# Second stage's short convolution: from diagonal matmuls to scaled evictions and GpSimd additions, with the first stage's weight loads issued ahead

## The chip, the cores and the metric

One core of a Trainium2 chip runs the whole program. The metric is device time in microseconds (us), the median of several runs. The engines are called as in the profile: PE (TensorE), DVE (VectorE), ACT (ScalarE), POOL (GpSimd), SP (SyncE, which here only issues DMAs). [...]

## What is computed

Four layers follow each other on an image tensor of 4 x 192 x 64 x 64, in fp32: a pair of mambas, a block with one mamba and a convolution, a convolution with weights made from the image, and a layer of sedenion products in 4 x 4 windows. The change touches the second layer's mamba, and a preparation of weights for the fourth layer. The mamba, cut to what matters (`xm` is 384 channels wide, D_CONV is 3, the convolution is per channel and causal):

```python
xz = jnp.einsum('blc,ec->ble', xf, in_proj_w)
xm, z = jnp.split(xz, 2, axis=-1)
conv = jax.lax.conv_general_dilated(xm_t, conv1d_w, (1,), [(D_CONV - 1, 0)],
    feature_group_count=D_INNER, dimension_numbers=('NCH', 'OIH', 'NCH'))
xm = jax.nn.silu(jnp.transpose(conv + conv1d_b[None, :, None], (0, 2, 1)))
x_dbl = jnp.einsum('bld,ed->ble', xm, x_proj_w)      # dt, B, C
delta = jax.nn.softplus(jnp.einsum('blr,dr->bld', dt, dt_proj_w) + dt_proj_b)
# h = exp(delta*A) * h + delta*xm*B ;  y = sum_n h*C  (a scan over the sequence)
y = ys + xm * Dskip
y = y * jax.nn.silu(z)
return jnp.einsum('bld,cd->blc', y, out_proj_w)
```

The first layer's two mambas have the same form with four taps.

## The kernel before

The program has three stages. `two_mambas` is the first layer. `mamba_block` is the second layer. `conv_and_windows` is the third and fourth.

**Units and ticks.** In the first two stages a unit is 512 positions of one sequence for one mamba: 64 units in the first stage, 32 in the second. Channels lie on the 128 partitions; 384 channels are three groups `d`. Of 384 x 16 states, 12 rows `k` of 4 tiles `j` are scanned one tile at a time (`step`, L574, DVE), so a unit is 48 scan steps. I call a scan step a tick. For each tile ACT makes the decay `dA` in PSUM (L568), two ticks ahead of the scan; three PSUM buffers hold it. For each row DVE forms the product with B (L561), and after its fourth tile POOL saves the state (L589) and multiplies by C (L590, `read`); four ticks later PE sums over the states (L599, `sum`). The `h` tiles have three buffers.

**What goes on behind the scan.** All other work is written as generators that yield a `Piece` ahead of each step, and the class `Behind` issues these steps between the ticks. It has four lanes, each a queue: lane 0 spreads C and runs `back` (output projection); lane 1 runs `front` of the next unit and then the first norm of the unit after; lane 2 runs `tail` (depthwise convolution, gelu, second norm); lane 3 runs `end` (the MLP). A piece states its PE time, the ticks to wait, what must be done first, whether it needs one of the two PSUM banks of that pool (`bank=True`), and whether it is a burst (an activation with another table, only allowed in one tick of four). Each tick adds 2.1 us of PE time to a budget in the second stage. A PSUM result's eviction is not issued with its matmul but through `later`, one tick on for ACT, two for DVE; its bank counts as held until then. The order of the instructions is thus fixed when the program is built; if data that a tick needs is not yet issued, `force` issues the lanes' steps until it is (the rows of the next unit are wanted at tick 36).

**The front before.** `front` projects the three groups with PE (L452, three banks), ACT copies each into `raw` behind two columns of the previous unit (`halo`, L448, L480), and nine matmuls with diagonal weights (`m_conv`, made at the start of the stage on DVE, L431) sum the three shifted copies in PSUM (L470, three banks). ACT evicts with the bias (L475) into `xc`, and a burst takes the silu over all three (L482). `xc` has two buffers; the convolution's pieces wait for `u["free"][:1]`, the flag that the unit before the present one has read its `xc` (set in tick 5). Then come the projection to dt, B and C (L486, L488), dt (L496, L499), its softplus (L505), its product with xc on POOL (L506), both stored to DRAM (`r_dt`, `r_dtx`, L511) from where `load` (L531) spreads the rows, and the gate z (L455, silu L523).

**Walsh weights.** `walsh_weights` runs once, at the start of the first stage, ahead of the first unit's front in SP's queue. For each of four pieces SP loads `w_raw` (L904; tag "h", three buffers), DVE takes four passes (L913, L923) between two result buffers (tag "h_apart"), and SP stores the result (L927).

Of the kernel before, what the change touches and what calls it, by code (L numbers as in the profile page):

```python
# [14 lines left out]
F32 = mybir.dt.float32  # L15
AF = mybir.ActivationFunctionType
ALU = mybir.AluOpType
# [5 lines left out]
C = 192  # L23
# [4 lines left out]
ND = DI // 128  # L28
# [4 lines left out]
T = 512  # L33
# [6 lines left out]
NP = NPOS // 2  # L40
# [134 lines left out]
class Behind:  # L175
# [19 lines left out]
        self.held += 1  # L195
        return self.psum.tile(shape, F32, name=name, tag="mm")

    def later(self, fn, dve=False, bank=True):
        done = [False]
        self.pending.append((self.now + (self.dve if dve else self.act), fn, done, bank))  # L200
        return done

    def issue(self, everything=False):
# [198 lines left out]
class Mamba:  # L402
# [1 line left out]


    def __init__(
        self, nc, name, taps, ins, const, last, scan, work, psum_y, psum_a, dram, ident, ex, behind, shared=()
    ):


        self.behind, self.y_free, self.shared = behind, True, shared
        self.nc, self.name, self.taps, self.ex = nc, name, taps, ex
        self.last, self.work, self.psum_y, self.psum_a = last, work, psum_y, psum_a
        self.dram = dram
        pack, pack_ap, in_w_ap, dt_w_ap = ins
        t = const.tile([128, pack.width], F32, name=f"{name}_pack")
        nc.sync.dma_start(t, pack_ap)
        w = pack.views(t)
        self.in_w = scan.tile([CP, 2, 2 * DI], F32, name=f"{name}_in_w")
        nc.scalar.dma_start(self.in_w, in_w_ap)  # L420
        self.dt_w = scan.tile([RK, DI], F32, name=f"{name}_dt_w")
        nc.scalar.dma_start(self.dt_w, dt_w_ap)
        self.conv_b, self.dt_b, self.D = w["conv_b"], w["dt_b"], w["D"]
        self.x_w, self.out_w = w["x_w"], w["out_w"]
        self.A = scan.tile([128, NQ, 4], F32, name=f"{name}_A")
        nc.scalar.activation(self.A, w["A_log"], AF.Exp)
        nc.vector.tensor_scalar_mul(self.A, self.A, -1.0)
        self.conv = scan.tile([128, ND, taps, 128], F32, name=f"{name}_conv")
        for d in range(ND):
            for j in range(taps):  # L430
                nc.vector.tensor_scalar_mul(  # L431
                    self.conv[:, d, j, :], ident, w["conv_w"][:, d, j : j + 1]
                )
        if shared:
            self.skip_w = scan.tile([128, ND, 128], F32, name=f"{name}_skip")
            for d in range(ND):
                nc.vector.tensor_scalar_mul(self.skip_w[:, d, :], ident, self.D[:, d : d + 1])
        self.halo = scan.tile([128, ND, taps - 1], F32, name=f"{name}_halo")
        self.state = scan.tile([128, NQ, 4], F32, name=f"{name}_state")

    def front(self, xn, first, u):


        nc, K, behind = self.nc, self.taps, self.behind
        raw = self.work.tile([128, ND, K - 1 + T], F32, name="raw", bufs=1)
        if first:
            nc.gpsimd.memset(self.halo, 0.0)
        nc.gpsimd.tensor_copy(raw[:, :, 0 : K - 1], self.halo)  # L448
        def project(e, to):
            ps = behind.bank([128, T], "ps_in")  # L450
            for k in range(2):
                nc.tensor.matmul(  # L452
                    ps, self.in_w[:, k, bass.ts(e, 128)], xn[:, k, :], start=(k == 0), stop=(k == 1)
                )
            return behind.later(lambda: nc.scalar.copy(to, ps))  # L455

        made = []
        for d in range(ND):
            yield Piece(1.7, bank=True)
            made.append(project(d, raw[:, d, K - 1 :]))  # L460
        halves = []
        for d in range(ND):
            for j in range(K):
                if j % 2 == 0:
                    yield Piece(1.7 if j < K - 1 else 0.85, bank=j == 0, after=made + u["free"][:1])
                if d == j == 0:
                    xc = u["xc"] = self.work.tile([128, ND, T], F32, name="xc", bufs=2)
                if j == 0:
                    ps = behind.bank([128, T], "ps_conv")
                nc.tensor.matmul(  # L470
                    ps, self.conv[:, d, j, :], raw[:, d, j : j + T], start=(j == 0), stop=(j == K - 1)
                )
            halves.append(
                behind.later(
                    lambda d=d, ps=ps: nc.scalar.activation(  # L475
                        xc[:, d, :], ps, AF.Identity, bias=self.conv_b[:, d : d + 1]
                    )
                )
            )
        nc.gpsimd.tensor_copy(self.halo, raw[:, :, T:])  # L480
        yield Piece(after=halves, burst=True)
        nc.scalar.activation(xc, xc, AF.Silu)  # L482
        yield Piece(2.6, bank=True, wait=2)
        ps = behind.bank([RK + 2 * NS, T], "ps_x")
# [4 lines left out]
        halves = []  # L489
        for d in range(ND):  # L490
            yield Piece(0.85, bank=True, after=[h], wait=0 if d else 3)
            if d == 0:
                dt = self.work.tile([128, ND, T], F32, name="dt", bufs=1)
                dtx = raw[:, :, K - 1 :]
            ps = behind.bank([128, T], "ps_dt")
            nc.tensor.matmul(ps, self.dt_w[:, bass.ts(d, 128)], dbl[:RK, :], start=True, stop=True)  # L496
            halves.append(
                behind.later(
                    lambda d=d, ps=ps: nc.scalar.activation(  # L499
                        dt[:, d, :], ps, AF.Identity, bias=self.dt_b[:, d : d + 1]  # L500
                    )
                )
            )
# [3 lines left out]
        rows = []  # L507
# [14 lines left out]
        yield Piece(after=made, burst=True)  # L522
        nc.scalar.activation(z, z, AF.Silu)  # L523
        u["silu"] = True

    def load(self, u, pair, i):

# [356 lines left out]
def walsh_weights(nc, work, w_ap, out):  # L884


    _, w_sign, _, _ = near_convolution()
    n = C // 2

    assert max(w_sign[:8]) < 0  # L890
    turns = [0] + [l for l in range(1, 8) if w_sign[8 + l] != w_sign[7 + l]] + [8]
    turns = list(zip(turns, turns[1:]))

    def flat(t):
        return t.rearrange("p a b -> p (a b)")[:, : 16 * n]

    def split(v, bit):
        return v.rearrange("p (h e l) -> p e h l", e=2, l=bit * n)

    for i in range(2):  # L900
        for at in range(0, C, n):
            raw = work.tile([128, 4, T], F32, name="w_raw", tag="h", bufs=3)
            v = flat(raw).rearrange("p (j c) -> p j c", c=n)
            nc.sync.dma_start(v, w_ap[:, i, :, at : at + n])  # L904
            t = [flat(work.tile([128, 4, T], F32, name="w_walsh", tag="h_apart", bufs=2)) for _ in range(2)]
            src = flat(raw)
            for m, bit in enumerate((8, 2, 1, 4)):
                a, dst = split(src, bit), t[m % 2]
                if bit == 8:
                    for first, last in turns:  # L910
                        at_l, ops = slice(n * first, n * last), (ALU.add, ALU.subtract)
                        for e, op in enumerate(ops[::-1] if w_sign[8 + first] > 0 else ops):
                            nc.vector.tensor_tensor(  # L913
                                split(dst, bit)[:, e, 0, at_l], a[:, 0, 0, at_l], a[:, 1, 0, at_l], op
                            )
                    src = dst
                    continue
                for e, op in enumerate((ALU.add, ALU.subtract)):
                    p, o = slice(0, 128), split(dst, bit)[:, e]
                    if i and bit == 4:  # L920
                        p = slice(64 * e, 64 * e + 64)
                        o = dst[p, : NP * n].rearrange("p (h l) -> p h l", h=2)
                    nc.vector.tensor_tensor(o, a[p, 0], a[p, 1], op)  # L923
                src = dst
            rows = slice(16, 16 + NP) if i else slice(0, 16)
            k = NP if i else 16
            nc.sync.dma_start(out[:, rows, at : at + n], src[:, : k * n].rearrange("p (j c) -> p j c", c=n))  # L927


def mamba_block(tc, x, p96, p96_ap, p128, p128_ap, m_in, ex_aps, out, sums, following):  # L930
# [4 lines left out]
    with ExitStack() as ctx:  # L935
# [18 lines left out]
        ln = NormT(nc, const, work, behind)  # L954
        ex = Expand(nc, fixed, *ex_aps)
        mamba = Mamba(
            nc, "m", 3, m_in, const, work, fixed, scan, psum_y, psum_a, dram, ln.ident, ex, behind
        )
        mlp = MlpT(nc, work, w["w1"], w["b1"], w["w2"], behind)

# [18 lines left out]
        def load(u):  # L979
            u["x"] = work.tile([CP, 2, T], F32, name="x", bufs=3)  # L980
            nc.sync.dma_start(
                u["x"], x[u["b"], :, bass.ts(u["t"], T)].rearrange("(k p) t -> p k t", p=CP)
            )
            u["loaded"][0] = True
# [780 lines left out]
```

## Time and profile before

| | |
|---|---|
| median of 3 runs | 10868.96 us (10867.93 to 10870.59) |
| the profiled execution | 10868.44 us |
| its span | 10866.7 us |
| busy, share of the span | PE 84%, DVE 84%, POOL 65%, ACT 60% |
| mean granted TensorE clock | 0.83 |
| first product of the first stage (DVE, L561) | starts at 91.35 us |
| first scans of the second stage | at 5435 us |
| one unit of the second stage | 105 to 126 us; eight follow in 901 us |
| DVE waiting for `w_raw` at the start (L913) | 22.7 us in three waits |

The page gives for each engine its busy time and, in 40 slices of 272 us, its busy share in tenths; the granted clock of TensorE stands below them in tenths of full speed. Groups of instructions are listed by source line with their count, busy time, mean duration in ns, and the idle time of the engine ahead of them with the instruction that ended it. A window's line gives its bounds and length, then PE, PEld (weight loads, beside the matmuls), DVE, ACT and POOL busy in it, the clock, the DMA share and GB/s. An fp32 matmul shows as two records. A busy PE is not PE at its peak.

### The profile page before, as it was taken

To read this page: it belongs to the slowest core of one execution; us is meant where nothing else is said; L and a number is where in the kernel's file an instruction comes from. 1 tells how busy PE (TensorE), PEld (TensorE's weight loads), DVE (VectorE), ACT (ScalarE), POOL (GpSimd) and SP (SyncE) were. 2 spreads that over 40 slices of the span, in tenths; PEclk is the share of its full clock that TensorE was granted. 3 is DMA by queue.
4 is the path that set the end of the run, shared out by engine and by line. 5 is a ranking of instruction groups with operands and counts; after the bars stand their busy time and mean duration, and the time that the engine had idled before them with its cause. 6 is when DMAs were issued, how large, how long until landed. Compare 5 with 4: busy or idle time off the path is not lost. (4 is left out here: it accounts for less than half of the span.)

```text
span 10866.7 us, 97590 instructions
## 1 busy us (share of the span) xinstructions
PE 9179.8 (84%) x31352; PEld 3644.1 (34%) x31352; DVE 9098.4 (84%) x7962; ACT 6566.6 (60%) x9784; POOL 7032.3 (65%) x2688
## 2 busy tenths in 40 slices
PE   6888878888887887887679999999999987889898
PEld 2222222222322222222223333333333333455555
DVE  7999999999999999999698888888888885555552
ACT  5666666666666666666466666656666663444443
POOL 5888888888888888888666656656656661111100
PEclk7777777777777777777678889889889887999999
DMA  5666666666666666666454545445444443122110
GB/s 158 177 181 180 177 177 183 175 176 182 177 177 179 177 178 179 176 178 180 128 151 135 140 127 143 133 125 141 129 134 133 133 121 82 41 50 64 42 40 18
DMA packets 969560, 1515.13 MB, mean 139 GB/s; under 512 B 244346, under 2 KB 277150, under 8 KB 968534
## 3 DMA queue, kind: packets, MB, share of 16 engines
q1 hardware_dynamic: 968190, 1505.85, 51.4%
q8 instruction: 247, 4.05, 0.2%
q10 hardware_dynamic: 856, 3.05, 0.1%
q14 instruction: 267, 2.19, 0.1%
HBM read 1295.45 MB, written 213.12 MB: 139 GB/s over the span
## 5 line engine op out<-in xcount | busy, mean ns | idle before, releaser
L574 DVE TENSOR_TENSOR_SCAN h<-dA,m_state,h 128x512 f32<-128x512 f32 x3840 | 4668.9, 1266 | 487.4 <-ACT dA L568 422.7
L590 POOL TENSOR_TENSOR h<-h,C 128x2048 f32<-128x2048 f32 x960 | 4345.4, 4531 | 621.6 <-ACT m_state L587 480.7
L568 ACT ACTIVATE dA<-dtE,m_A 128x512 f32<-128x512 f32 x4608 | 3106.1, 687 | 1332.9 <-DVE h L574 1227.8
L561 DVE TENSOR_TENSOR h<-dtxE,B 128x2048 f32<-128x2048 f32 x960 | 2170.6, 2261 | 78.6 <-DMA dtxE<-r_dtx 65.9
L599 PE MATMUL y<-h,gather 128*32 128x512 f32 x7680 | 1281.3, 746 | 422.9 <-POOL h L590 345.2
L452 PE MATMUL ps_in<-xT,m_in_w 96*128 96x512 f32 x1536 | 939.5, 759 | 258.6 <-ACT raw L455 127.1
L1300 POOL TENSOR_TENSOR d<-d,rs 128x512 f32<-128x512 f32 x64 | 86.8, 1357 | 1589.7 <-DVE rs L1299 1569.1
L470 PE MATMUL ps_conv<-raw,m_conv 128*128 128x512 f32 x2112 | 989.3, 617 | 1.7 <-ACT xc L475 1.7
L574 DVE TENSOR_TENSOR_SCAN h_apart<-dA,m_state,h_apart 128x512 f32<-128x512 f32 x768 | 922.3, 1260 | 40.0 <-ACT dA L568 40.0
L590 POOL TENSOR_TENSOR h_apart<-h_apart,C 128x2048 f32<-128x2048 f32 x192 | 870.2, 4532 | 39.7 <-ACT m_state L587 38.0
L561 POOL TENSOR_TENSOR h_apart<-dtxE,Bs 128x2048 f32<-128x2048 f32 x192 | 889.6, 4633 | 6.0 <-ACT Bs L550 6.0
L452 PEld LDWEIGHTS ps_in<-xT,m_in_w 96*128 96x128 f32 x1536 | 351.3, 241 | 827.2 <-issue 420.5
L589 POOL COPY m_state<-h 128x4 f32<-128x4 f32 x384 | 72.3, 188 | 849.5 <-DVE h L574 813.5
L470 PEld LDWEIGHTS ps_conv<-raw,m_conv 128*128 128x128 f32 x2112 | 417.9, 202 | 599.0 <-issue 562.4
L1049 PE MATMUL ps_dw<-strip,dw 96*96 96x512 f32 x1152 | 578.7, 650 | 1.3 <-ACT x L1058 0.9
L599 PEld LDWEIGHTS y<-h,gather 128*32 128x32 f32 x7680 | 164.7, 117 | 1225.4 <-POOL h L590 552.0
L506 POOL TENSOR_TENSOR raw<-dt,xc 128x1536 f32<-128x1536 f32 x96 | 330.0, 3437 | 294.6 <-ACT dt L505 294.6
L486 PE MATMUL ps_x<-xc,m_pack 128*44 128x512 f32 x576 | 351.0, 758 | 199.5 <-ACT xc L482 194.6
L1465 PE MATMUL sed_ps<-xn,sed 64*128 64x256 f32 (+3 forms) x2944 | 485.9, 404 | 7.0 <-DVE y L1484 7.0
L568 ACT ACT_TABLE_LOAD x345 | 442.6, 1283 | 28.5 <-DMA dtE<-r_dt 22.3
L452 PE MATMUL ps_in<-xn,m_in_w 96*128 96x512 f32 x768 | 399.0, 666 | 47.4 <-ACT z L455 31.2
L378 PE MATMUL ps_o<-hid,t 128*96 128x512 f32 x768 | 390.4, 647 | 34.3 <-ACT hid L371 13.0
(193 smaller groups left out, 12217.1 us busy)
## 6 DMA issues: line engine op xcount, KB each, us to landing
dtE<-r_dt SPq DMA_DIRECT2D x2304, 256.0 KB, 5.0
dtxE<-r_dtx SPq DMA_DIRECT2D x2304, 256.0 KB, 4.1
r_dt<-dt SPq DMA_DIRECT2D x96, 768.0 KB, 4.0
r_dtx<-raw SPq DMA_DIRECT2D x96, 768.0 KB, 5.4
x<-x SPq DMA_DIRECT2D x64, 384.0 KB, 3.9
img<-x SPq DMA_DIRECT2D x28, 512.0 KB, 8.2
xt<-in_x SPq DMA_DIRECT2D x32, 384.0 KB, 5.8
x<-o SPq DMA_DIRECT2D x32, 384.0 KB, 5.0
```

What stands on the lines that cost most here:

```text
L378: nc.tensor.matmul(ps, self.w2[:, m, bass.ts(k, CP)], h[:, m, :], start=(m == 0), stop=(m == NH - 1),)
L452: nc.tensor.matmul(ps, self.in_w[:, k, bass.ts(e, 128)], xn[:, k, :], start=(k == 0), stop=(k == 1))
L470: nc.tensor.matmul(ps, self.conv[:, d, j, :], raw[:, d, j : j + T], start=(j == 0), stop=(j == K - 1))
L486: nc.tensor.matmul(ps, self.x_w[:, d, :], xc[:, d, :], start=(d == 0), stop=(d == ND - 1))
L506: nc.gpsimd.tensor_tensor(dtx, dt, xc, ALU.mult)
L561: engine.tensor_tensor(h, u["rows", k // 2, 1], u[B, k % 2].unsqueeze(1).broadcast_to([128, 4, T]), ALU.mult)
L568: self.nc.scalar.activation(dA, u["rows", k // 2, 0][:, j, :], AF.Exp, scale=self.A[:, k, j : j + 1])
L574: self.nc.vector.tensor_tensor_scan(h[:, j, :], u.pop(("dA", k, j)), h[:, j, :], self.state[:, k, j : j + 1], ALU.mult, ALU.add,)
L590: nc.gpsimd.tensor_tensor(h, h, u["C", k % 2].unsqueeze(1).broadcast_to([128, 4, T]), ALU.mult)
L599: self.nc.tensor.matmul(u["ys"][32 * j : 32 * j + 32, :], self.ex.gather[:, i // 2, :], h[:, j, :], start=(i == 0), stop=(i == 3 and not s ...
L1049: nc.tensor.matmul(ps, dw[:, k, j, :], s[:, k, dy : dy + rows, dx : dx + HW], start=(j == 0), stop=(j == 8),)
L1465: nc.tensor.matmul(out, sed[p, int(h is not None), i ^ position(k, s), cols], xn[b, g][p, c, :], start=group(t) not in begun, stop=left[gr ...
```

## The change

In the second stage only (`summed=True`), the convolution no longer goes through PE. Each projection's PSUM bank is evicted three times by ACT, each time multiplied by one tap's weight per channel: tap 0 into `raw`, tap 1 into a new tile `one` (it shares the buffer of `dt`), tap 2 with the bias into `xc`. The three evictions of a bank are issued in three following ticks (`more=j`), and the bank counts as held until the third. POOL then adds the shifted `raw` and the shifted `one` to `xc`, each over 128 x 1536 elements. `halo` keeps three columns: two of tap 0, one of tap 1. The projections now wait for the free `xc`. The first stage keeps the matmuls, moved word for word into `convolve`. The Walsh weights' loads are issued three at once ahead of the loop, the fourth after the first piece.

```diff
-    def later(self, fn, dve=False, bank=True):
+    def later(self, fn, dve=False, bank=True, more=0):
         done = [False]
-        self.pending.append((self.now + (self.dve if dve else self.act), fn, done, bank))
+        self.pending.append((self.now + (self.dve if dve else self.act) + more, fn, done, bank))
...
+        self.conv_w = w["conv_w"]
+        if not summed:
+            self.conv = scan.tile([128, ND, taps, 128], F32, name=f"{name}_conv")
...
-        self.halo = scan.tile([128, ND, taps - 1], F32, name=f"{name}_halo")
+        self.halo = scan.tile([128, ND, taps if summed else taps - 1], F32, name=f"{name}_halo")
...
+        if self.summed:
+            yield from self.sum_taps(raw, projected, u)
+        else:
+            yield from self.convolve(raw, project, u)
+        xc = u["xc"]
         nc.scalar.activation(xc, xc, AF.Silu)
...
+    def sum_taps(self, raw, projected, u):
+        nc, behind = self.nc, self.behind
+        halves = []
+        for d in range(ND):
+            yield Piece(1.7, bank=True, after=u["free"][:1])
+            if d == 0:
+                xc = u["xc"] = self.work.tile([128, ND, T], F32, name="xc", bufs=2)
+                one = self.work.tile([128, ND, 1 + T], F32, name="one", tag="dt", bufs=1)
+                nc.gpsimd.tensor_copy(one[:, :, 0:1], self.halo[:, :, 2:])
+            ps = projected(d)
+            for j, o in enumerate((raw[:, d, 2:], one[:, d, 1:], xc[:, d, :])):
+                bias = {"bias": self.conv_b[:, d : d + 1]} if j == 2 else {}
+
+                def tap(o=o, ps=ps, d=d, j=j, bias=bias):
+                    nc.scalar.activation(o, ps, AF.Identity, scale=self.conv_w[:, d, j : j + 1], **bias)
+
+                h = behind.later(tap, bank=(j == 2), more=j)
+            halves.append(h)
+        yield Piece(after=halves, wait=2)
+        nc.gpsimd.tensor_copy(self.halo[:, :, :2], raw[:, :, T:])
+        nc.gpsimd.tensor_copy(self.halo[:, :, 2:], one[:, :, T:])
+        nc.gpsimd.tensor_tensor(xc, xc, raw[:, :, :T], ALU.add)
+        yield Piece(wait=2)
+        nc.gpsimd.tensor_tensor(xc, xc, one[:, :, :T], ALU.add)
+        yield Piece(burst=True, wait=4)
...
+    pieces = [(i, at) for i in range(2) for at in range(0, C, n)]
+    raws = [load(*p) for p in pieces[:3]]
+    for made, (i, at) in enumerate(pieces):
+        if made and made + 2 < len(pieces):
+            raws.append(load(*pieces[made + 2]))
+        raw = raws[made]
...
         mamba = Mamba(
-            nc, "m", 3, m_in, const, work, fixed, scan, psum_y, psum_a, dram, ln.ident, ex, behind
+            nc, "m", 3, m_in, const, work, fixed, scan, psum_y, psum_a, dram, ln.ident, ex, behind, summed=True
         )
```

## The prediction

> **What bounds the kernel now.** I read the page's slices first, then the costliest groups, then windows cut out of the second stage, last the waits there and the timeline of the start. One sure measure to begin with: 0.2% of this time, 22 us, is about what a measurement can tell from no change.
>
> The slices and groups of the page:
> ```profile
> PE   6888878888887887887679999999999987889898
> DVE  7999999999999999999698888888888885555552
> POOL 5888888888888888888666656656656661111100
> PEclk7777777777777777777678889889889887999999
> ...
> L574 DVE TENSOR_TENSOR_SCAN h<-dA,m_state,h 128x512 f32<-128x512 f32 x3840 | 4668.9, 1266 | 487.4 <-ACT dA L568 422.7
> L590 POOL TENSOR_TENSOR h<-h,C 128x2048 f32<-128x2048 f32 x960 | 4345.4, 4531 | 621.6 <-ACT m_state L587 480.7
> L568 ACT ACTIVATE dA<-dtE,m_A 128x512 f32<-128x512 f32 x4608 | 3106.1, 687 | 1332.9 <-DVE h L574 1227.8
> L470 PE MATMUL ps_conv<-raw,m_conv 128*128 128x512 f32 x2112 | 989.3, 617 | 1.7 <-ACT xc L475 1.7
> ```
> Slices 1 to 19 are the first stage: DVE at 9, PE at 8, so DVE sets the time. Slices 21 to 32 are the second stage: PE at 9 nearly throughout and DVE at 8. There the convolution is PE work: 32 units x 9 matmuls x 2 records of the 2112 (the first stage has 1536).
>
> [...]The starts of the scans in the trace give units of 105 to 126 us in a pattern that repeats every 8 units (901 us, 112.6 us each). I cut eight units into rows 0 to 2, 3 to 7 and 8 to 11. The sums and means of these three answers, in this order (stretch, then PE, PEld, DVE, ACT, POOL):
> ```profile
> sum 196.10, PE 191.00 PEld 73.10 DVE 177.72 ACT 111.21 POOL 137.91; mean PE 23.87 PEld 9.14 DVE 22.22 ACT 13.90 POOL 17.24
> sum 423.40, PE 392.79 PEld 123.77 DVE 308.05 ACT 271.27 POOL 241.53; mean PE 49.10 PEld 15.47 DVE 38.51 ACT 33.91 POOL 30.19
> sum 281.60, PE 245.75 PEld 109.39 DVE 263.09 ACT 186.60 POOL 169.83; mean PE 30.72 PEld 13.67 DVE 32.89 ACT 23.33 POOL 21.23
> ```
> Per unit: rows 0-2 take 24.5 us, DVE idle 2.3; rows 3-7 take 52.9, DVE idle 14.4; rows 8-11 take 35.2, DVE idle 2.3. The same windows for the convolution's line alone show all of it in rows 0-2: 8.16 us of PE in each of the eight. So the work that goes lies where DVE is idle only 2.3 us; the large idle time lies later. Half of the eight units pass rows 0-2 in 21.9 to 22.1 us (21.9 and 25.3 stand side by side below), with the convolution in them:
> ```profile
> 7413.90:7439.20 25.30, 25.07 (x74) 9.11 (x73) 21.68 (x16) 15.99 (x24) 18.52 (x12) 1.00 0.48 127
> 7519.50:7541.40 21.90, 21.90 (x63) 8.68 (x62) 21.59 (x17) 12.41 (x21) 15.94 (x12) 1.00 0.47 123
> ```
> What DVE waits for in the second stage, from the waits between 5600 and 8600 us:
> ```profile
> DVE h L574 <- ACT dA L568: 317.4, 189, 6.0
> ...
> POOL raw L506 <- ACT dt L505: 221.4, 27, 15.1
> ...
> ACT xc L475 <- PE ps_conv L470: 86.2, 76, 2.5
> ```
> ACT takes its queue in order; an eviction that waits for PE holds up the next dA, and dA runs only two ticks ahead of the scan. That is how a late PE reaches DVE.
>
> [...]weight loads of one accumulation are 0.85 us apart in one place and 0.43 in the next; mean clock of the eight windows is 0.97 in rows 0-2, where PE is densest, and 0.81 in rows 8-11. So PE work taken out can lower the clock. [...]The trace: copy 586, with one pointer 687, with scale and bias (L1058) 773.
>
> **The change, part by part.**
>
> *Start.* Before, each w_raw load is issued behind the store of the previous piece, so DVE waits 8.07, 7.96 and 6.64 us (22.7 together). After, three loads are out at once. A piece costs DVE 2.4 + 5.6 = 8.0 us. A result buffer is still read by its store (landing 3.9 us) when the next piece wants it after 2.4 us: 1.5 us late, three times. Walsh ends near 20.0 + 32 + 4.5 = 57 instead of 74.7. SP then no longer holds r_dt (75.2) and r_dtx (75.8) behind the last store; what is late next is POOL's dtx, done at 64.6. r_dtx goes 11 us earlier and with it the first product (91.35). DVE bounds stage one, so I keep **-11 us** (bounds -7 to -14; three loads beside xt could cost some).
>
> *Exposed front of unit 0 and constants.* Nine diagonal products, 9 x 0.2 us of DVE, go; the mean (PE, 5372.4) is then what is late, gain about 0.6. The front: 7.9 us of convolution and an eviction against two POOL adds of 3.44; the silu would start at 5402.2 instead of 5402.85. Together **-1**.
>
> *PE, each of 31 units behind the scan:* -8.16 us, all in rows 0-2. The projections move: they now wait for the free xc buffer (the skip of the previous unit, tick 5), which the convolution waited for before; they go out at ticks 5, 5 and 8 instead of 0 to 2. DVE's 22.2 us remains. The densest units without a late eviction stay 0.3 above it; I take 0.7 above, 22.9: **-1.6** (bounds 0 and -2.3).
>
> *Rows 3-7.* Nothing is removed there. But the silu of xc (two table loads of 1.28 and 1.48: 4.05 us of ACT) leaves ticks 9 or 13, where it now delays the hid evictions that PE's ps_out waits for. In the unit from 7173.7 this cost PE 2.75 us and DVE's strip 3.84 at 7204. It goes to tick 17, among the depthwise matmuls, where the dA behind it are as exposed. I take **-1.5** for the backlog that PE no longer brings into row 3 and **+0.3** for the silu's new place (bounds -4 and +4; no trace shows it there).
>
> *ACT:* six evictions (3 x 0.586 + 3 x 0.687 = 3.8 us) become nine (6 x 0.687 + 3 x 0.773 = 6.4): +2.6 us in ticks 6 to 11, where ACT has 13.9 us of work in 24.5. Two taps a tick beside a dA make 2.1 us against DVE's 1.85: **+0.3**.
>
> *POOL:* two adds of the dtx size (3.437) and two halo copies (0.19): +7.3 us in ticks 11 to 13. POOL has 137.91/8 = 17.2 of 24.5 us in rows 0-2. Queue: read of row 2 (0.19 + 4.53), add, strip copies (0.8), add: 12.4 us from the end of row 2. The read of row 3 stands behind and is some 4 us late; its sum on PE is due four ticks later with 2.4 us of slack. The silu, due five ticks later (9 to 13 us), may wait a little on ACT. **+0.5** (bounds 0 and +5).
>
> *Latency of the front:* silu at 17, softplus at the burst slot 25 (before 21 or 25), rows at 28; they are wanted at tick 36, so nothing is forced: 0. The first tap bank is held three ticks instead of one, but three banks instead of six are used: 0. Stage three is untouched: 0.
>
> Sum: -1.6 - 1.5 + 0.3 + 0.3 + 0.5 = -2.0 us a unit; x 31 = -62; with -11 and -1: **-74**. The profiled execution took 10868.4 (span 10866.7), the median is 10869.0; I predict **10795**.
>
> **Rivals.**
>
> *A, the sum above* (0.50): 10795. Its own range: -0.4 to -4.7 a unit, 10845 to 10710. For it: PE busy 92% (829 of 901 us) in the stage. Against it: DVE's small idle time where the convolution is.
>
> *B, hidden* (0.16): DVE bounds rows 0-2, nothing is gained later; only the start and 0 to -0.3 a unit, 10848 to 10868. For it: the 21.9 us units.
>
> *C, POOL's adds become the wait* (0.22). The two adds stand in POOL's queue ahead of the read of row 3, and the silu in ACT's queue behind them, with dA behind the silu. Should the last tap reach POOL late by more than the 2.5 us that dA runs ahead, DVE stops for the rest, and PE's sum of row 3 too. Price up to 5 us; with the -2.5 of the other terms +2.5 to +3 a unit: 31 x 3 - 12 = +81, **10950**. For it: dtx already costs POOL 8 us of waiting a unit (221.4/27). It decides from about 2.5 us net loss a unit.
>
> *D, the clock* (0.12): rows 0-2 get the clock of rows 8-11 (0.81) and carry it into row 3. A clock of 0.86 instead of 0.91 over 49.1 us of PE work costs 2.9 a unit, net +0.9: 10885, slower only just.
>
> That the convolution's matmuls stay is excluded by the diff; that the loads do not go ahead could be if the store of the first piece still stood before them, but three are issued before the loop.
>
> **How the numbers follow.** Faster: A and a little of B, 0.52. Within 0.2% (10847 to 10891): B and part of D, 0.16. Slower: C, the rest of D, 0.32. Signs are mixed, so the range takes A's own 10710 at the low end and reaches into C at the high end: 10710 to 10930, with about 0.08 below and 0.12 above.
>
> **What would show it.** L470 at 1536 records; POOL 64 more 128x1536 additions near 3.44; first product near 80 us; rows 0-2 near 22.9 us with PE near 16 to 19. C shows as PE y <- POOL h and ACT xc <- POOL xc waits of several us in rows 3-4. D shows as a clock below 0.9 in rows 3-7. I am wrong if rows 0-2 stay at 24, or if rows 3-7 grow beyond 53.

## The result, and the profile after

The kernel after takes 10860.8 us in the median of four runs (10859.7 to 10862.6), the kernel before 10869.8 beside it (10867.9 to 10871.0): ratio 0.9992, 95% interval 0.9975 to 1.0009. That is no change that can be measured. The prediction was 10795.

From the page of the kernel after, the busy slices and the groups that answer to those of before (line, engine, operation, tiles, count | busy us, mean ns | idle before, released by):

```profile
PE   7888888888888887887678889889888986889898
...
DVE  8999999999999999999698888888888885555552
...
POOL 6888888888888888888676666666676661111100
PEclk7777777777777777777678988888898887899999
...
L619 DVE TENSOR_TENSOR_SCAN h<-dA,m_state,h 128x512 f32<-128x512 f32 x3840 | 4673.6, 1266 | 409.6 <-ACT dA L613 345.9
L635 POOL TENSOR_TENSOR h<-h,C 128x2048 f32<-128x2048 f32 x960 | 4347.4, 4534 | 605.3 <-ACT m_state L632 500.8
L613 ACT ACTIVATE dA<-dtE,m_A 128x512 f32<-128x512 f32 x4608 | 3108.4, 687 | 1468.6 <-DVE h L619 1370.2
...
L531 PE MATMUL ps_conv<-raw,m_conv 128*128 128x512 f32 x1536 | 727.9, 625 | 0.0
```

The work did go: `ps_conv` has the first stage's 1536 records left. In slices 21 to 32 PE's digits dropped a little, so did the clock's, and DVE's 8 stayed: the pace of the scans hardly changed.

Where the time went, from the first and last scans of both traces:

| stretch | before | after |
|---|---|---|
| start to the first scan | 93.8 us | 79.2 (-14.6) |
| scans of the first stage | 5239.4 | 5240.4 |
| change of stages | 102.3 | 98.5 (-3.8) |
| first to last scan of the second stage | 3520.4 | 3507.1 (-13.3) |
| last scan to the end | 1910.8 | 1934.6 (+23.8) |

The same eight units, cut into rows 0-2, 3-7 and 8-11 by the scans of the trace after (three answers; stretch, busy time of each engine, then means of a unit):

```profile
sum 224.00, PE 179.07 PEld 67.12 DVE 184.23 ACT 157.67 POOL 128.53; mean PE 22.38 PEld 8.39 DVE 23.03 ACT 19.71 POOL 16.07
sum 391.00, PE 374.31 PEld 121.65 DVE 309.05 ACT 256.41 POOL 280.47; mean PE 46.79 PEld 15.21 DVE 38.63 ACT 32.05 POOL 35.06
sum 275.90, PE 230.75 PEld 97.06 DVE 256.93 ACT 171.77 POOL 191.84; mean PE 28.84 PEld 12.13 DVE 32.12 ACT 21.47 POOL 23.98
```

Rows 0-2 take 28.0 us instead of 24.5, rows 3-7 48.9 instead of 52.9, rows 8-11 34.5 instead of 35.2: a unit went from 112.6 to 111.4. The rows that lost 8.16 us of convolution have only 1.5 us less PE in them, and ACT has 19.7 us there instead of 13.9. A part of this is the lower clock (mean of the eight windows 0.87 instead of 0.97 in these rows), at which a matmul takes longer: in the slow window below, the projection's weight loads are 0.43 us apart ahead of a wait of 7.0 us, at a granted clock of 1.00 (7170.3 to 7174.0), and 0.86 after it, at 0.50 (7182.0 to 7185.5). The larger part is other work: 18 PE records a unit went, but only 3 fewer are there (65.6 instead of 68.5). Cut to the tile `hid`, ACT's share of the MLP in these rows went from 1.50 to 4.37 us a unit (before, then after): other lanes' steps moved in.

```profile
sum 196.10, ACT 12.00; mean ACT 1.50
```
```profile
sum 224.00, ACT 34.98; mean ACT 4.37
```

Two of the windows, one slow and one fast, with 22.2 and 15.9 us of ACT (bounds, length, then PE, PEld, DVE, ACT and POOL with their counts, clock, DMA):

```profile
7157.70:7187.10 29.40, 22.41 (x68) 8.67 (x67) 23.18 (x17) 22.18 (x31) 16.35 (x13) 0.86 0.35 91
...
7497.60:7521.50 23.90, 21.96 (x55) 7.87 (x54) 21.97 (x17) 15.91 (x26) 15.98 (x12) 0.87 0.33 88
```

What DVE waited for between 5600 and 8600 us (us, times, longest; first one line of before, then after):

```profile
DVE x L1084 <- PE ps_o L378: 9.4, 8, 3.4
```
```profile
DVE h L619 <- ACT dA L613: 246.9, 219, 6.2
DVE x L1136 <- PE ps_o L378: 86.1, 31, 3.9
DVE strip L1072 <- PE ps_out L1063: 79.0, 50, 4.9
```

The wait for the decays fell from 317 to 247. The wait of the MLP's last sum `x` for its matmul `ps_o`, 9.4 us (8 times) before, is new at this size, and took that gain back. PE's largest new wait is for the third tap, which holds the projection's bank, and POOL waits less for dt:

```profile
PE ps_in L457 <- ACT xc L559: 128.2, 24, 7.0
```
```profile
POOL raw L496 <- ACT dt L495: 56.8, 27, 2.4
```

### The profile page after: what moved, and what is told of

Read it like the earlier page. It is cut to its first block, busy times and chain, and to the rows that moved or that the text cites. A ratio compares the mean times of both kernels' runs of the same rounds, so it can differ in the third digit from the quotient of the medians.

```text
span 10859.9 us, 96522 instructions
## 1 busy us (share of the span) xinstructions
PE 9009.0 (83%) x30776; PEld 3561.5 (33%) x30776; DVE 9102.4 (84%) x7953; ACT 6632.6 (61%) x9880; POOL 7240.8 (67%) x2816
## 5 line engine op out<-in xcount | busy, mean ns | idle before, releaser
L606 DVE TENSOR_TENSOR h<-dtxE,B 128x2048 f32<-128x2048 f32 x960 | 2169.4, 2260 | 67.1 <-DMA dtxE<-r_dtx 67.1
L1352 POOL TENSOR_TENSOR d<-d,rs 128x512 f32<-128x512 f32 x64 | 86.1, 1345 | 1613.2 <-DVE rs L1351 1592.7
L635 POOL TENSOR_TENSOR h_apart<-h_apart,C 128x2048 f32<-128x2048 f32 x192 | 870.7, 4535 | 38.7 <-ACT m_state L632 37.4
L531 PE MATMUL ps_conv<-raw,m_conv 128*128 128x512 f32 x1536 | 727.9, 625 | 0.0
L457 PE MATMUL ps_in<-xn,m_in_w 96*128 96x512 f32 x768 | 473.1, 767 | 230.4 <-ACT xc L559 148.2
L1101 PE MATMUL ps_dw<-strip,dw 96*96 96x512 f32 x1152 | 529.6, 609 | 1.6 <-ACT x L1110 0.9
L531 PEld LDWEIGHTS ps_conv<-raw,m_conv 128*128 128x128 f32 x1536 | 312.5, 207 | 449.4 <-issue 419.7
L359 PE MATMUL ps_h<-xn,t 96*128 96x512 f32 x768 | 429.6, 715 | 15.0 <-ACT xn L337 9.8
```

The lines of the kernel that those rows point to most:

```text
L359: nc.tensor.matmul(ps, self.w1[:, k, bass.ts(m, 128)], x[:, k, :], start=(k == 0), stop=(k == 1))
L457: nc.tensor.matmul(ps, self.in_w[:, k, bass.ts(e, 128)], xn[:, k, :], start=(k == 0), stop=(k == 1))
L531: nc.tensor.matmul(ps, self.conv[:, d, j, :], raw[:, d, j : j + T], start=(j == 0), stop=(j == K - 1))
L606: engine.tensor_tensor(h, u["rows", k // 2, 1], u[B, k % 2].unsqueeze(1).broadcast_to([128, 4, T]), ALU.mult)
L635: nc.gpsimd.tensor_tensor(h, h, u["C", k % 2].unsqueeze(1).broadcast_to([128, 4, T]), ALU.mult)
L1101: nc.tensor.matmul(ps, dw[:, k, j, :], s[:, k, dy : dy + rows, dx : dx + HW], start=(j == 0), stop=(j == 8),)
```

## The experiments

Each run had the kernel before beside it on the same chip (10866 to 10870 us); differences below are to that. Unless said otherwise the edits are to the kernel after.

**The parts.** Walsh loads alone (`summed=True` left off; run e1):

> The changed kernel with summed left off: only the Walsh loads ahead. In the changed kernel the first scan starts 14.6 us earlier (79.2 instead of 93.8). Theory S (a start gain lasts to the end, since DVE bounds stage one): 10869.8 - 14 = 10855 to 10857, ratio 0.9987. Rival L (the gain is absorbed before the end, by the third stage or the change of stages): 10866 to 10870, ratio 1.000.

10852.3, -13.9 us, ratio 0.9987 (0.9981 to 0.9994). The start lasts to the end. So about +5 is left for the convolution's part, too little to tell from nothing.

POOL's adds left out (e3):

```diff
-        nc.gpsimd.tensor_tensor(xc, xc, raw[:, :, :T], ALU.add)
...
-        nc.gpsimd.tensor_tensor(xc, xc, one[:, :, :T], ALU.add)
```

> The changed kernel without POOL's two adds, same ticks (left out: taps 0 and 1 of the convolution never reach xc). Theory H: POOL's adds are beside other work, the time falls by less than 0.5 us a unit, 10845 to 10861. Rival P: row 3 (13.9 us now) falls by 2 us or more, total 10800 or less.

10825.3, -40.9, between the two expectations. So the adds cost some 32 us in the medians, and 23 between the two traces (the profiled run, 10838.7, is the slowest of five). A steady unit changed by 0.4 us only (111.35 to 110.95); unit 0 went from 104.2 to 97.8 and the change of stages from 98.5 to 93.2, where they stand exposed.

TensorE's work: in the kernel before, three of nine matmuls, everything else issued in the same order (e4).

```diff
+                if K == 3 and j:
+                    continue
                 nc.tensor.matmul(
...
```

> The kernel before with three instead of nine convolution matmuls in the second stage, same pieces, budgets and order of everything else (left out: taps 1 and 2 of the convolution). It takes away 6/9 of 8.16 us, 5.4 us of PE a unit, with no other edit. Theory B (hidden: DVE bounds rows 0-2): at most 1 us a unit, 10840 to 10870, rows 0-2 at 23.5 or more. Rival R (PE sets the pace of rows 0-3, as my sum assumed: -1.6 and -1.5): -2 to -4 us a unit, 10750 to 10805.

10797.2, -69.0, ratio 0.9937 (0.9924 to 0.9949). Taking 5.4 us of matmuls a unit out of the densest rows is worth 2.2 us a unit in the mean, although DVE seemed to leave no room there: the theory that it is hidden falls.

ScalarE's work: the Walsh run with six Identity instructions a unit whose results nobody reads, meant for ticks 5 to 8 (e12), then all issued with the first product (e13).

```diff
+                for n in [2 * d + j // 2] if K == 3 and j != 1 else []:
+                    nc.scalar.activation(one[:, n % 3, :], raw[:, n % 3, 2:], AF.Identity)
```

> The Walsh loads ahead and the convolution as before (run e1), plus six Identity instructions of 128x512 per unit on ScalarE, one at each half of the three diagonal products (ticks 5 to 8), into a tile that nobody reads: ScalarE's share of the change alone, TensorE's work and the order of all else untouched. Theory A (ScalarE, which hands DVE its decays in order, has no room in rows 0 to 2: what stands in its queue there delays the decays): 10930-11050, that is half to all of 6 x 0.7 us x 32 units on top of 10852. Theory P (ScalarE has room, it idles a third of the time; only TensorE's order matters): 10850-10880.

> As run e12, but the six Identity instructions all at the first half of the first product (tick 5). Theory A: slower than e12 by 30 us or more, since six in a row hold back the decays by 4 us at a stroke where three dA buffers bridge one step or two. Theory P: 10850-10880. If e12 and e13 agree and both are slow, it is the amount and not the spacing.

10852.0 (-17.1) and 10872.5 (+3.3). Spread, six more instructions a unit cost nothing (between 5500 and 8700 us ACT has 173 more than in e1 and is busy 84.8 us longer, some 3.0 us a unit); at one place they cost 20 us. The trace of e13 has most of these in a single unit, the fourth of the stage (123.8 us instead of 109.2 in e1); eight steady units take 112.6 us each in e1 and e13 alike. Theory A falls as to amount. As to spacing it shows a cost in a few units, below the 30 us that it named, and none in a steady unit.

**The order.** The kernel before, its nine matmuls kept, only the projections made to wait for the free `xc` as the change makes them (e7), and this with three of nine matmuls (e8):

```diff
-            yield Piece(1.7, bank=True)
+            yield Piece(1.7, bank=True, after=u["free"][:1] if K == 3 else ())
             made.append(project(d, raw[:, d, K - 1 :]))
```

> The kernel before, all nine matmuls kept, with its projections in the second stage waiting for the free xc as in the change (tick 5), so that the rest of the front comes as late as there. Theory O: slower, since 8.16 us of PE a unit at the price of e4_one_tap (65 us for 5.4 a unit, so about 100 for 8.16) should have come out of the change and 10 came: 10940 to 11000, and the stretch after the last scan near 1934. Rival B' (in the late order PE's work in these rows is free): 10866 to 10890.

> As e7_before_late with three of the nine matmuls (left out: taps 1 and 2 of the convolution). Against e7_before_late it prices 5.4 us of PE a unit in the late order. Theory O: 50 to 75 us less, as in the early order (69). Rival B': less than 20 us.

10980.2, +110.8, ratio 1.0102 (1.0088 to 1.0116). With the products in place this is the largest single effect of the change, and nothing in it is work. With three of nine matmuls 10856.3: in this order the same 5.4 us of PE are worth 124 us, more than expected. The waits of the first of the two, against 9.4 us of the second kind before:

```profile
DVE h L574 <- ACT dA L568: 263.5, 219, 5.0
DVE x L1084 <- PE ps_o L378: 124.4, 22, 6.0
```

If the late projections were all, starting them early again should have paid. A third `xc` buffer and no wait (e5); then also all taps of a bank at once (e6); and taps at once in the late order (e2):

```diff
-            yield Piece(1.7, bank=True, after=u["free"][:1])
+            yield Piece(1.7, bank=True)
...
-                xc = u["xc"] = self.work.tile([128, ND, T], F32, name="xc", bufs=2)
+                xc = u["xc"] = self.work.tile([128, ND, T], F32, name="xc", bufs=3)
```
```diff
-                h = behind.later(tap, bank=(j == 2), more=j)
+                h = behind.later(tap, bank=(j == 2))
```

> The changed kernel with a third xc buffer and no wait of the projections for a free xc: they go out from tick 0 on again, the silu at 13 instead of 17. Theory O (the late start of the front gave the gain back: it moved the silu and the projection to dt into the depthwise matmuls[...]): rows 0-2 fall from 28.0 to 24.5 or less, the total to 10780 to 10820. Rival H (the three evictions that hold a bank): 10850 or more, since the hold is unchanged. Both leave the stretch after the last scan at about 1934 us (1911 before), because the same pieces are still open at the end of the scans.

> As e5_early, and the three evictions of a bank in one tick. Theory O: within 10 us of e5_early. Rival H: 40 us or more below e5_early. If both count, they add: e5_early less 8, what the same edit gave the changed kernel.

> The changed kernel with more=j left off: the three scaled evictions of a bank go out in one tick and the bank counts as held for one tick instead of three. Theory H (the long hold is the cost: PE idles before the third projection on ACT's third tap, 128 us in 27 units, and goes to half clock after it): the wait PE ps_in <- ACT xc falls below 40 us, rows 0-2 fall from 28.0 to 24.5 us or less, 10770 to 10800. Rival P (POOL's two adds and the silu behind them are the cost): rows 0-2 and the total stay, 10855 to 10865. Rival A (three taps of 0.7 us at once in ACT's queue hold up dA): slower, DVE waits for dA grow beyond 247 us, 10880 or more.

10886.0 (+16.6), 11025.0 (+155.6) and 10853.2 (-13.0). The gain of theory O (the late start is the cost) did not come: early projections leave the convolution's ticks open instead, and MLP steps fill those (4.65 us of `hid` on ACT in rows 0-2, against 1.50 before); DVE waits 116.8 us for `ps_o`. Theory H (the long hold of the bank is the cost) falls too. Taps at once in the late order cut PE's wait for the third tap from 128.2 to 98.0 us, yet eight steady units take the same 111.4 us each. In the early order taps at once cost 139 us; why is not settled.

Next the place of the convolution itself was kept: projections at ticks 0 to 2, taps read from `raw` in SBUF at ticks 5 to 7, silu at tick 9 or 13 (e10); then with that place open to other lanes (e11); then e10 without the adds (e14).

```diff
+            nc.scalar.activation(xc[:, d, :], raw[:, d, 2:], AF.Identity, scale=w[:, d, 2:3], bias=bias)
...
+            nc.scalar.activation(one[:, d, :T], raw[:, d, 1 : 1 + T], AF.Identity, scale=w[:, d, 1:2])
...
+            nc.scalar.activation(raw[:, d, :T], raw[:, d, :T], AF.Identity, scale=w[:, d, 0:1])
```

> The sum of taps in the order of the kernel before: three projections at ticks 0 to 2 copied to raw as before, at ticks 5 to 7 in place of the diagonal products ScalarE reads raw from SBUF (xc with the third tap and the bias, one with the second, raw itself in place with the first: nine Identity instructions), POOL adds twice, silu at tick 9 or 13. Each third of the convolution keeps 1.7 us of its budget as a blank. ScalarE has six instructions more than in the kernel before, three more than in the kernel after. Theory F and theory L both: 10740-10800, since neither the filling nor the lateness is there and 8.2 us of TensorE work per unit is gone (three ninths of it left gave -69 us in the early order). Theory N (the new work of ScalarE and POOL costs as much as TensorE's saves, wherever it stands): 10845-10900.

> The run e10 with no budget kept: the ticks of the convolution are open to other lanes, which bring MLP steps there; silu still at tick 9. Theory F: slower than e10 by 30 us or more, the wait of DVE for ps_o over 60 us. Theory L: within 20 us of e10. Theory N: 10845-10900.

> Run e10 without POOL's two adds (left out: the sum of the taps). In e10 ScalarE waited 79 us in the window 5600 to 8600 for the adds (silu stands at tick 9, two ticks behind them), against 0 in the kernel after (silu at tick 17). Theory A: 10900-11000, the nine evictions at ticks 5 to 7 remain; theory D (POOL's adds ahead of an early silu were the wait): 10780-10850.

11043.9 (+175.4), 11222.4 (+354) and 10862.6 (-6.5). Theory F (freed ticks are filled, and that costs) and theory L (lateness costs) both miss e10 by 240 us or more, theory N by 144. Opening the place to other lanes (e11 against e10) came as F says: 178 us slower, and DVE's wait for `ps_o` rose from 6.1 to 84.4 us. The adds cost 181 us in this place; without them the time lies between the two expectations. ACT's waits in the first of the three, and two lines of its timeline, show the rival of the prediction that POOL's adds would become the wait (a timeline line has start, duration, the instruction, and in brackets the idle time ahead of it):

```profile
ACT xc L471 <- POOL xc L564: 79.1, 23, 7.3
```
```profile
7534.27 1.48 ACT L471 ACTIVATE xc<-xc 128x1536 f32<-128x1536 f32 x1 [7.34 <-POOL xc L564]
...
7537.79 1.28 DVE L615 TENSOR_TENSOR_SCAN h<-dA,m_state,h 128x512 f32<-128x512 f32 x1 [6.51 <-ACT dA L609]
```

The silu waits for POOL's adds, and the decays are issued behind the silu. In this trace ACT stood 7.34 us for the add, the decays came only after the silu, and the next scan waited 6.51 us for them. The kernel after has no such wait: its silu comes at tick 17. That a late silu is the price of having the adds fits this, but no run moved the silu alone. A late PE reaches DVE in the same way in the trace before: ACT stood 5.96 us for `ps_dw` ahead of its eviction `x` (L1058, 7232.56 us), the decay came after that (7233.24), and the scan at 7233.95 had waited 4.75 us for it.

Last, the extra evictions of the change itself: the no-adds kernel (e3) with its six extra evictions cut to two columns each (e15).

> Run e3 (the kernel after without POOL's adds, 10825) with the six extra evictions cut to their last two columns (left out: most of the first and the second tap), so that ScalarE and POOL have little more than in the kernel before and TensorE its 8.2 us less per unit, in the order of the kernel after. Theory A: 6 x 0.5 us x 32 units at half to full price, 10730-10780. Theory L (the late order alone costs): 10810-10830.

10855.0 (-14.1), 27 slower than with full evictions. Less work, more time: rows 0-2 got 1.3 us shorter, row 7 1.8 us longer, and the wait for `ps_o` went from 78.6 to 130.2. Theory A's number was missed by 75 us, theory L's by 25.

**Blanks.** Three steps that issue nothing, where the projections had been; below for the kernel after (e9), the late kernel before (e16), and both with blanks of 0.85 us (e17, e18):

```diff
         for d in range(ND):
+            yield Piece(1.7, bank=True)
+        for d in range(ND):
             yield Piece(1.7, bank=True, after=u["free"][:1])
```

> The kernel after with one edit: ahead of its three projections the front has three blank steps of 1.7 us each that issue nothing, so that no other lane fills ticks 0 to 2 with the last unit's MLP, as it does in the kernel after; the projections stay where they are (from tick 5). Theory F (the freed ticks are filled with MLP steps, and DVE, which sets the pace, then waits for their ps_o: 86 us in the window 5600 to 8600 against 9 before): the wait for ps_o falls back under 30 us and the time to 10780-10820. Theory L (the lateness of the front itself is what costs: silu at tick 17 in place of 9 or 13, and all behind it eight ticks later): it stays at 10845-10900, whatever the wait for ps_o does.

> Run e7 (the kernel before with its projections late, all nine matmuls, 10980) plus the three blank steps of 1.7 us that e9 added to the kernel after. Theory F (the ticks 0 to 4 that the late projections leave open are filled with MLP steps, and that is what costs): 10880-10930, the blanks give back 45 us or more as they did in e9. Theory L (late is late: silu and all behind it come eight ticks later): 10965-11000. Theory U (each change of the order moves the time by tens of us either way, by where steps happen to meet, and e9 was a good draw): no direction, a number outside both is as likely as within.

> Run e9 with blanks of 0.85 us instead of 1.7. Theory F: between the kernel after (10861) and e9 (10816), 10825-10850, since half the room is kept free. Theory U: as likely outside of that interval as in it.

> The kernel e17 with the nine diagonal products back in place of the taps (Walsh loads ahead, projections late, three blanks of 0.85 us): what the exchange of products for taps itself is worth at equal rules of order. At full blanks it was worth nothing: e9 at 10816, e16 at 10832 less the 14 us of the Walsh loads. Theory Z (the exchange is worth nothing, the order is all): 10800-10825, within 15 us of e17's 10808. Theory R (8.2 us of TensorE work a unit is worth its 60 to 120 us, e17 shows it and e9 hid it): 10870-10930.

| three blanks of | nine products | taps and adds |
|---|---|---|
| none | 10980.2 (+110.8) | 10860.8 (-9.0), Walsh ahead |
| 1.7 us | 10831.6 (-38.7) | 10815.8 (-52.7), Walsh ahead |
| 0.85 us | 10892.4 (+22.7), Walsh ahead | 10808.0 (-62.2), Walsh ahead |

Blanks help in all four comparisons: 150 us and some 74 with products (14 for the Walsh loads taken off), 44 and 53 with taps. In the kernel before they take the wait for `ps_o` from 124.4 us to this:

```profile
DVE h L576 <- ACT dA L570: 352.3, 178, 4.9
DVE x L1086 <- PE ps_o L378: 22.0, 14, 2.5
```

Did the blanks keep the MLP out of rows 0-2, as theory F has it? ACT's time on `hid` there tells (us a unit over eight steady units; DVE's wait for `ps_o` is that between 5600 and 8600 us):

| run | ACT on `hid` in rows 0-2 | length of rows 0-2 | wait for `ps_o` |
|---|---|---|---|
| kernel before | 1.50 | 24.5 | 9.4 |
| products late, no blank (e7) | 5.31 | 29.3 | 124.4 |
| products, 0.85 us (e18) | 5.22 | 29.8 | 23.9 |
| products, 1.7 us (e16) | 1.77 | 23.5 | 22.0 |
| taps, no blank (after) | 4.37 | 28.0 | 86.1 |
| taps, 0.85 us (e17) | 5.06 | 29.1 | 72.1 |
| taps, 1.7 us (e9) | 3.10 | 25.2 | 67.2 |

The sums behind the first column, for e7 and then e16:

```profile
sum 234.70, ACT 42.48; mean ACT 5.31
```
```profile
sum 188.40, ACT 14.20; mean ACT 1.77
```

With products and full blanks the MLP steps, the rows and the wait all go back. That supports theory F as to direction, though the time fell below its interval; theory L falls, since the front is as late as in e7. With taps and full blanks the MLP goes back in part only. With half blanks it stays in rows 0-2, these rows get no shorter, and the time falls by some 74 and 53 us all the same: theory F does not explain that. In e17, 14 of the 17 us that eight steady units gain over the kernel after lie in one of them (128.1 to 114.4 us). Half the blank also gave more than the whole one, outside of theory F's interval.

Down a column of the first table, then, the order alone moves the time by up to 150 us; along a row the exchange of products for taps is worth -105, 0 and -85 (14 for the Walsh loads taken off the first two). The last of these is a run of its own (e18 against e17), and came as theory R there says.

The clock differs in the row with the 0. Between 5500 and 8700 us: first products late, then taps, then products and taps with full blanks, then products and taps with half blanks (after PE, PEld, DVE, ACT, POOL comes the granted clock):

```profile
5500.00:8700.00 3200.00, 2919.45 (x8550) 1063.35 (x8549) 2635.91 (x2047) 1976.63 (x2620) 1934.59 (x1040) 0.86 0.50 132
```
```profile
5500.00:8700.00 3200.00, 2794.56 (x8308) 1014.32 (x8307) 2712.02 (x2110) 2099.53 (x2789) 2174.08 (x1189) 0.85 0.51 136
```
```profile
5500.00:8700.00 3200.00, 2896.74 (x8925) 1056.13 (x8924) 2738.77 (x2135) 2061.42 (x2734) 2015.51 (x1085) 0.93 0.51 138
```
```profile
5500.00:8700.00 3200.00, 2836.94 (x8408) 1004.84 (x8406) 2736.11 (x2132) 2123.11 (x2821) 2198.29 (x1201) 0.86 0.52 138
```
```profile
5500.00:8700.00 3200.00, 2949.37 (x8730) 1079.16 (x8728) 2682.09 (x2087) 2007.62 (x2669) 1968.79 (x1062) 0.87 0.51 134
```
```profile
5500.00:8700.00 3200.00, 2775.26 (x8432) 1004.30 (x8431) 2755.55 (x2141) 2134.88 (x2838) 2207.61 (x1208) 0.87 0.53 138
```

With unit times of 115.2, 111.4, 110.1, 108.5, 112.6 and 109.2 us, PE is busy 105.1, 97.2, 99.6, 96.2, 103.8 and 94.7 us a unit (its busy time x unit / 3200). Without blanks and with half ones the clock stayed (0.86 to 0.85, 0.87 to 0.87), and the exchange saved 7.9 and 9.1 us of busy PE. With full ones it stood at 0.93 and fell to 0.86, and only 3.4 were saved. So products and clock went together in one pair of three; that the clock is the cause of the 0 is an inference.

The best version is the kernel after with three blanks of 0.85 us: 10808.0, ratio to before 0.9942 (0.9929 to 0.9956). It beats both kernels.

## Why the prediction was wrong

**The sum has a missing term.** Three numbers describe the -9 that was measured where -74 was expected: Walsh loads -14 (run alone), the late place of the projections +111 (run alone in the kernel before), and the exchange of products for taps in that place -105. The last is no run of its own but what is left, so that the three must add up. The prediction had -11, 0 and -62, with -1 for the change of stages.

The split depends on the order in which it is made: with taps, the late kernel is not slower than the early one (e5, with a third `xc` buffer) but 25 us faster. What was missed can be seen in the kernel after itself: three empty steps where the projections had been bring 44 to 53 of the missing 65 us.

- *Latency of the front, 0, "nothing is forced"*: the step that failed, by 111 us in the kernel before. The move of the projections was put at nothing because the rows would come in time. They did: DVE's waits for the rows of dt x xc are 67.1 us over the whole program, 65.9 before. But steps that move free the ticks they leave, and the rules of the order give them at once to whoever waits, here MLP steps (`hid` in rows 0-2 from 1.50 to 5.31 us a unit in e7, and to 4.37 in the kernel after). The prediction listed each moved step and asked who waits for it; it did not ask who takes its place. How much of the 44 to 53 us in the kernel after goes through this filling stays open.
- *Rows 0-2, -1.6*: they got slower by 3.5 us. The bound ("22.2 us of DVE remains") held, but rows without convolution are not rows without PE and ACT. Nor were the fast units half of the eight: three of them passed in 21.9 to 22.1 us. "I am wrong if rows 0-2 stay at 24" was the right place to look.
- *Rows 3-7, -1.5 + 0.3*: measured -4.0; right in sign and too small. Rows 8-11 gave another -0.7. Together a steady unit got 1.3 us shorter instead of 2.0.
- *Times 31*: this multiplication failed as well. The steady 1.3 us would be -40; the scans of the stage gained 13. Unit 0, where POOL's adds are exposed, got 6.2 us longer, units 1 to 7 together 3.5, and the last two units 4.8. After the last scan 24 us came back. The late kernel before, with all its products, has the same 1935.1 us after its last scan, so that belongs to the order of the last units, not to the exchange; which step of it was not settled (e5, with early projections, has 17 of the 24).
- *ACT, +0.3*: 0 when spread, and 0 in a steady unit even when bunched (e12, e13). Small, as expected.
- *POOL, +0.5*: 0.4 in a steady unit, right; the adds measured 3261 and 3076 ns (expected 3437). The exposed copies of unit 0 and the change of stages, put inside a -1, were the larger part.
- *Start, -11*: -14.6, just beyond its bounds. The last Walsh store was issued at 57.4 us (57 in the sum), with 5.5 us of waits for the result buffers instead of 4.5; the first product came at 76.8 instead of near 80.
- *Rival C* did not come in the kernel after, where PE's wait for POOL's `h` is 23.0 us with the adds and 22.4 without them (e3; 2.8 in the kernel before). It came in full in e10, where the silu was early (+181 us for the adds). *Rival D* in its own words fell: rows 3-7 went up from 0.91 to 0.95. But the clock of the stage as a whole went from 0.89 to 0.85: rows 0-2 fell from 0.97 to 0.87 and rows 8-11 from 0.81 to 0.72. *Rival B* had the right time (10848 to 10868) by luck: PE's work is not hidden (-69 and -124 us).

**What stays open.** Why blanks pay where the MLP stays in rows 0-2, why half a blank is better than a whole one with taps and worse with products, why taps at once cost 139 us in one order, and the 24 us of the last units. The runs show that an order as such can be worth as much as the work exchanged; a rule for the best order they don't give.

## What to carry over

When a change moves steps in an order that fills itself, first build the kernel before with the move alone: that one run is worth more than a sum of instruction costs. Ask of each freed slot what will flow into it, not only who waits for what has moved; steps that issue nothing are a cheap thing to try, but look in the trace whether they kept the slot free or helped in another way. Taking work off one engine can pay where that engine's lateness reaches the pace setter, even in stretches where the pace setter looks busy throughout: with DVE at work in 22.2 of 24.5 us, 5.4 us of PE less a unit brought 69 us (e4).

## What was not expected of the hardware

The granted clock of TensorE went with the order of the steps at least as much as with the products. The prediction held that it can fall when products go, an estimate from 0.97 in rows 0-2, where PE is densest, and 0.81 in rows 8-11 before. At full blanks it did fall: nine products a unit less brought it from 0.93 to 0.86, and busy PE fell by 3.4 us a unit instead of 8.2. Without blanks and at half blanks it moved by 0.01 or less, and in the kernel before, six of nine products less (e4) took it from 0.89 to 0.88. Moving the projections alone (e7) took it from 0.89 to 0.86.

And in rows where ACT works 13.9 of 24.5 us, six more instructions, some 3.0 us of busy ACT a unit, cost nothing if spread (e12): 10852.0 against 10852.3 us.
